# Where a weight table's comparisons run: VectorE or GpSimd

## The chip, the cores and the metric

The kernel runs on one core of a Trainium2 chip. A core has five engines that run side by side, each with its own instruction queue: TensorE (PE, matrix products), VectorE (DVE), ScalarE (ACT), GpSimd (POOL) and SyncE (SP, here the issuer of all transfers). The metric is the device time of one execution in microseconds; before the change its median is 2431.11 us over 3 runs (2429.63 to 2433.48).

## The reference, cut to what matters

Two "macaron" transformer layers act on x of 1024 tokens by 256 features. Each layer is a half-weighted feed-forward, an attention, and the same feed-forward again. The second layer's feed-forward does not store its weights: each weight is one of 16 values of a table `lut`, chosen by an index.

```
def _ghost_linear(x, idx, lut):
    w = lut[idx]
    return jnp.einsum('bsh,oh->bso', x, w)
gate = _ghost_linear(x, gate_idx, lut)
up = _ghost_linear(x, up_idx, lut)
h = jax.nn.silu(gate) * up
return _ghost_linear(h, down_idx, lut)

x = x + 0.5 * L0_ffn(layernorm(x))
x = x + L0_attn(layernorm(x))        # 16 heads of 128, window of 64, differential softmax, rope
x = x + 0.5 * L0_ffn(layernorm(x))
x = x + 0.5 * L1_ffn(layernorm(x))   # the table weights above
x = x + L1_attn(layernorm(x))        # gated delta rule
x = x + 0.5 * L1_ffn(layernorm(x))
```

The gate and up indices are 256 by 688, the down index 688 by 256 (padded to 768 rows in the kernel).

## The kernel before, in words

All of x stays in SBUF as eight tiles of 128 tokens. Matrix products work on 512 tokens at a time (a "half"). The layers follow each other in program order. Within each engine a planner at build time has laid out one fixed order of instructions, moving some of them past each other, and the engines synchronise by semaphores.

**The tables.** `lut_weights` (L169) is a Python generator that builds the three weight matrices `w1g`, `w1u` and `w1d`. It takes 14 pieces: for each of the two 128-row blocks of gate and up, one of 512 columns and one of 176, and for down six blocks of 256 columns. For each piece it loads the int32 index tile `ix` (two buffers, a transfer of SyncE, L178). Then, for each of the 16 table values k, one instruction compares all indices with k and multiplies the result by the value `lk` (L183, on VectorE); its output `eq` (three buffers) is added to the piece on GpSimd (L185). For k = 0 the comparison writes the piece itself and there is no addition. This makes 224 comparisons (64 of 512 columns, 64 of 176, 96 of 256) and 210 additions (60, 60 and 90).

**Where the steps go.** `lut_steps(columns)` advances the generator until about so many columns have been emitted. It is called after each of the 12 inner chunks of the first feed-forward with 1024, and after each chunk of attention with 1536, so the table work is spread behind the first feed-forward and the first attention. What is left is emitted after attention. The tables are read first in the fourth of the six parts.

**Around them.** In the first feed-forward, TensorE makes `pg` and `pu` (L135), ScalarE applies silu (L140), VectorE multiplies into `hT` (L143), TensorE makes `po` (L160) and VectorE adds it to x (L167). Then the layernorm runs on VectorE (L106 to L116) with transposes on TensorE and copies on ScalarE. The attention makes the values `v` (L212, copied by ScalarE in L219, shifted by transfers in L220 and L222). For each of four head groups it then makes one key and four query ropes per half of the tokens, ten in all: a product `pr` (L228, two buffers), three VectorE instructions (L237, L238, L240) and one GpSimd addition of `rot` (two buffers) in L241. After that come eight chunks per head group: scores `ps` on TensorE (L277), their maximum on VectorE (L288), exponentials on ScalarE (L294), the difference `d` of two softmaxes (L311, L314, two buffers), and its normalisation on GpSimd (L321). Transposes, the product with `v` and the output product end a chunk (L324, L329, L340, L347). GpSimd thus has attention's L241 and L321 in the same queue as the table additions.

After the attention come the remaining feed-forwards and the delta rule, which takes most of the span and has no table work.

Of the kernel before, what the change touches and what calls it, by code (L numbers as in the profile page):

```python
# [14 lines left out]
ALU = mybir.AluOpType  # L15
# [42 lines left out]
def macaron_kernel(ctx, tc, out, a):  # L58
    nc = tc.nc
# [109 lines left out]
    def lut_weights(pool):  # L169

        for src, dst in (("gate_idx", w1g), ("up_idx", w1u), ("down_idx", w1d)):
            for c in range(dst.shape[1]):
                for c0 in range(0, dst.shape[2], 512):
                    n = min(512, dst.shape[2] - c0)
                    ix = pool.tile([P, n], I32, name="ix", tag="ix", bufs=2)
                    nc.sync.dma_start(out=ix, in_=a[src][c * P : (c + 1) * P, c0 : c0 + n])  # L178
                    acc = dst[:, c, c0 : c0 + n]
                    for k in range(NLUT):  # L180
                        lk = bc[:, B_LUT + k : B_LUT + k + 1]
                        to = acc if k == 0 else pool.tile([P, n], F32, name="eq", tag="eq", bufs=3)
                        nc.vector.tensor_scalar(to, ix, float(k), lk, ALU.is_equal, ALU.mult)  # L183
                        if k:
                            nc.gpsimd.tensor_add(acc, acc, to)  # L185
                        yield n
# [164 lines left out]
    with tc.tile_pool(name="w0", bufs=1, side="right") as w0p:  # L351
# [12 lines left out]
        with tc.tile_pool(name="wa", bufs=1) as wap, tc.tile_pool(  # L364
# [19 lines left out]
            for i in range(2):  # L384
                nc.sync.dma_start(
                    out=wa["lam"][i * 64 : (i + 1) * 64, :], in_=lams[i].partition_broadcast(64)
                )
            lut = lut_weights(lutp)
            with ExitStack() as st:
                pools = stage_pools(st)  # L390
# [506 lines left out]
```

## Time and profile before

| | |
|---|---|
| median of 3 runs | 2431.11 us |
| profiled execution, own time | 2426.46 us |
| its span | 2424.6 us |
| busy TensorE, VectorE, ScalarE, GpSimd | 2093.0, 1431.5, 896.1, 854.9 us |
| comparisons L183 on VectorE | 175.65 us, from 39.9 to 276 us |
| first rope addition on GpSimd (L241) | 188.4 us |
| last table addition ends | 277.3 us |
| mean granted TensorE clock | 0.911 |

The page gives busy times of engines over one execution. A group line names the source line, the engine, the operation, output and inputs, the shapes and the count, and then the busy time, the mean of one in ns, and the engine's idle time before it with what ended it. The timeline gives start, duration and the number of merged instructions, with the idle time before in brackets. The windows view cuts the span into stretches and gives each engine's busy time there, the granted clock, and the share and rate of transfers.

### The profile page before, as it was taken

How to read it: one execution, taken by the hardware profiler on the slowest of the kernel's cores; microseconds unless marked ns; L12 is line 12 of the kernel's file. 1: busy time of each engine (PE TensorE's matmuls, PEld its weight loads, DVE VectorE, ACT ScalarE, POOL GpSimd, SP SyncE). 2: the span in 40 equal slices, each digit the busy share in tenths (PEclk: the TensorE clock that was granted, in tenths of full speed). 3: DMA queues.
4: the chain of work that ended last, by engine and by line, in shares of the span. 5: the costliest groups of instructions: out<-in, count | busy, mean ns of one | idle time of the engine just before them, and what ended most of it. 6: DMA issues, size and time to landing. Idle time of an engine off the chain costs nothing. (4 is left out here: it accounts for less than half of the span.)

```text
span 2424.6 us, 33184 instructions
## 1 busy us (share of the span) xinstructions
PE 2093.0 (86%) x12640; PEld 1714.2 (71%) x12640; DVE 1431.5 (59%) x3036; ACT 896.1 (37%) x1960; POOL 854.9 (35%) x995
## 2 busy tenths in 40 slices
PE   8535888878987898999889999799999979999989
PEld 4212554554546898888788888688888968888864
DVE  5999765553335565665655656556565655655541
ACT  2012453462233434343443343443434344343330
POOL 3887522210003334343243334334334233342320
PEclk9777898989997998999899989899998988988999
DMA  5010000000000000000000000000000000000000
GB/s 178 12 45 5 11 1 0 9 31 0 1 0 1 1 1 1 27 5 5 10 1 1 10 23 1 14 1 1 1 19 14 1 14 1 1 1 1 1 1 18
DMA packets 19182, 28.52 MB, mean 12 GB/s; under 512 B 2768, under 2 KB 11664, under 8 KB 18768
## 3 DMA queue, kind: packets, MB, share of 16 engines
q1 hardware_dynamic: 19024, 26.40, 3.5%
q8 instruction: 101, 1.65, 0.3%
q14 instruction: 57, 0.47, 0.1%
HBM read 23.38 MB, written 1.05 MB: 10 GB/s over the span
## 5 line engine op out<-in xcount | busy, mean ns | idle before, releaser
L652 PE MATMUL pm<-kq,k 128*128 128x128 f32 x1792 | 303.3, 302 | 90.8 <-POOL k L670 85.7
L670 POOL TENSOR_TENSOR k<-k,d 128x256 f32<-128x256 f32 x192 | 181.1, 943 | 497.9 <-PE pm L652 496.6
L699 PE MATMUL dz<-zt,mz 128*128 128x64 f32 x1792 | 342.5, 283 | 3.2 <-ACT mz L687 3.2
L652 PEld LDWEIGHTS pm<-kq,k 128*128 128x128 f32 x1792 | 254.4, 207 | 113.8 <-POOL k L670 104.7
L687 ACT COPY mz<-pmz 128x512 f32<-128x512 f32 x224 | 130.9, 584 | 502.7 <-PE pmz L685 502.7
L692 PE MATMUL dz<-mz,zt 128*128 128x64 f32 x1536 | 302.1, 279 | 5.1 <-ACT mz L687 4.8
L699 PEld LDWEIGHTS dz<-zt,mz 128*128 128x128 f32 x1792 | 279.6, 201 | 6.1 <-ACT mz L687 4.7
L685 PE MATMUL pmz<-z,mt 128*128 128x128 f32 x1792 | 271.9, 297 | 1.9 <-DVE z L709 1.9
L692 PEld LDWEIGHTS dz<-mz,zt 128*128 128x128 f32 x1536 | 248.4, 199 | 25.5 <-ACT mz L687 13.4
L685 PEld LDWEIGHTS pmz<-z,mt 128*128 128x128 f32 x1792 | 246.2, 209 | 10.8 <-DVE z L709 8.4
L664 DVE TENSOR_TENSOR kq<-kq,d 128x512 f32<-128x512 f32 x192 | 160.2, 835 | 126.5 <-PE pm L652 118.5
L709 DVE TENSOR_TENSOR z<-z,dz 128x256 f32<-128x256 f32 x192 | 80.7, 420 | 179.5 <-PE dz L699 178.9
L183 DVE TENSOR_SCALAR eq<-ix,bc 128x256 f32<-128x256 int32 (+2 forms) x210 | 165.9, 838 | 1.2 <-POOL w1g L185 0.4
L294 ACT ACTIVATE e<-ps,nm 128x128 f32<-128x128 f32 x256 | 90.6, 373 | 86.5 <-DVE nm L289 82.9
L680 DVE COPY_PREDICATED qk<-kon,pm 128x256 f32<-128x256 int32 x224 | 114.1, 510 | 0.0
L560 DVE SCALAR_TENSOR_TENSOR k<-ps,pp,k 128x256 f32<-128x256 f32 x192 | 87.2, 476 | 42.4 <-ACT k L558 40.4
L711 DVE TENSOR_TENSOR zt<-zt,dz 128x256 f32<-128x256 f32 x224 | 92.9, 415 | 28.4 <-PE dz L699 27.6
L560 DVE SCALAR_TENSOR_TENSOR v<-ps,pp,v 128x256 f32<-128x256 f32 x192 | 88.5, 478 | 15.5 <-ACT v L558 13.9
L560 DVE SCALAR_TENSOR_TENSOR q<-ps,pp,q 128x256 f32<-128x256 f32 x192 | 89.7, 479 | 13.3 <-ACT q L558 10.2
L546 PE MATMUL ps<-xnT,wk 128*128 128x259 f32 x256 | 77.6, 424 | 20.0 <-DVE k L560 20.0
L679 DVE TENSOR_TENSOR mt<-pm,kon 128x256 f32<-128x256 f32 x224 | 92.7, 414 | 0.0
L228 PE MATMUL pr<-xnT,wq 128*128 128x512 f32 x128 | 64.0, 629 | 29.4 <-DVE kT L240 27.0
(183 smaller groups left out, 4159.6 us busy)
## 6 DMA issues: line engine op xcount, KB each, us to landing
wq<-in_aWq SPq DMA_DIRECT2D x1, 2048.0 KB, 14.8
wo<-in_aWo SPq DMA_DIRECT2D x1, 2048.0 KB, 18.9
wk<-in_dWk SPq DMA_DIRECT2D x4, 512.0 KB, 3.8
wq<-in_dWq SPq DMA_DIRECT2D x4, 512.0 KB, 3.6
wv<-in_dWv SPq DMA_DIRECT2D x4, 512.0 KB, 3.6
wdo<-in_dWo SPq DMA_DIRECT2D x4, 512.0 KB, 3.8
v<-v SPq DMA_DIRECT2D x15, 128.0 KB, 2.3
x<-in_x SPq DMA_DIRECT2D x4, 256.0 KB, 3.2
```

What stands on the lines that cost most here:

```text
L183: nc.vector.tensor_scalar(to, ix, float(k), lk, ALU.is_equal, ALU.mult)
L560: nc.vector.scalar_tensor_tensor(yh, xi, pp[:, col : col + 1], yh, ALU.mult, ALU.add)
L652: nc.tensor.matmul(pm[:, h].rearrange("p b (s l) -> p b s l", l=n), lhsT=k[:, h, :], rhs=kq[:, :, h, :].rearrange("p b (s two l) -> p b s ...
L664: nc.vector.tensor_mul(kqr, kqr, dl.unsqueeze(1).unsqueeze(3).to_broadcast([P, 2, HG * runs, n]),)
L670: nc.gpsimd.tensor_mul(kl, kl, dr.unsqueeze(2).to_broadcast([P, HG * runs, n]))
L679: nc.vector.tensor_mul(dst(mt), src(0), mask4)
L680: nc.vector.copy_predicated(dst(qk), heads(mask.bitcast(I32)).rearrange("p h (s l) -> p h s l", l=n), src(1))
L685: nc.tensor.matmul(pmz[:, h, :], lhsT=mt[:, h, :], rhs=z[:, h, :], start=True, stop=True)
L687: nc.scalar.copy(mz, pmz)
L692: nc.tensor.matmul(dz[:, 0, h, :].rearrange("p (s l) -> p s l", l=n), lhsT=zt[:, h, :], rhs=left(mz[:, h, :], n), start=True, stop=True,)
L699: nc.tensor.matmul(dz[:, 1, h, :].rearrange("p (s l) -> p s l", l=n), lhsT=mz[:, h, :], rhs=right(zt[:, h, :], n), start=True, stop=True,)
L711: nc.vector.tensor_sub(zr, zr, runs4(dz[:, 1]))
```

## The change

The comparison with multiplication (L183) is issued on GpSimd in place of VectorE. Piece sizes, buffers, index loads, additions and the calls of `lut_steps` stay.

```
                     for k in range(NLUT):
                         lk = bc[:, B_LUT + k : B_LUT + k + 1]
                         to = acc if k == 0 else pool.tile([P, n], F32, name="eq", tag="eq", bufs=3)
-                        nc.vector.tensor_scalar(to, ix, float(k), lk, ALU.is_equal, ALU.mult)
+                        nc.gpsimd.tensor_scalar(to, ix, float(k), lk, ALU.is_equal, ALU.mult)
                         if k:
                             nc.gpsimd.tensor_add(acc, acc, to)
                         yield n
```

In the built program, VectorE's queue has no table instruction left. GpSimd's queue has the comparison of step k+1 between the additions of steps k-1 and k. The first rope addition L241 now stands behind 58 comparisons and 53 additions of 512 columns and 48 and 45 of 176 (before: behind 60 additions of 512, 60 of 176 and 23 of 256); the six first L321 of the first head group still stand before the end of the tables.

More of the change, by code (lines that the diff above doesn't have):

```diff
@@ L182, in lut_weights @@
                         to = acc if k == 0 else pool.tile([P, n], F32, name="eq", tag="eq", bufs=3)
-                        nc.vector.tensor_scalar(to, ix, float(k), lk, ALU.is_equal, ALU.mult)
+                        nc.gpsimd.tensor_scalar(to, ix, float(k), lk, ALU.is_equal, ALU.mult)
                         if k:
```

## The prediction

> **What bounds the kernel now.** The page says TensorE is busy 86% of the span, but the change acts only on the tables, so I first asked where they are built. The grouped list by shape for GpSimd, cut to 40 to 293 us, holds all of its table work (columns: count, busy us, mean ns, idle before it and what ended that):
>
> ```profile
> L185 POOL TENSOR_TENSOR w1d<-w1d,eq 128x256 f32<-128x256 f32 x90 | 66.2, 736 | 13.3 <-DVE eq L183 6.1 <-DVE nm L289 1.4 <-DVE lw L307 0.3
> L185 POOL TENSOR_TENSOR w1u<-w1u,eq 128x512 f32<-128x512 f32 x30 | 40.7, 1356 | 3.6 <-DVE eq L183 1.8
> L185 POOL TENSOR_TENSOR w1g<-w1g,eq 128x512 f32<-128x512 f32 x30 | 40.2, 1341 | 44.0 <-DVE eq L183 42.2
> L185 POOL TENSOR_TENSOR w1g<-w1g,eq 128x176 f32<-128x176 f32 x30 | 17.5, 582 | 2.6 <-DVE eq L183 0.6
> L185 POOL TENSOR_TENSOR w1u<-w1u,eq 128x176 f32<-128x176 f32 x30 | 17.1, 571 | 2.3 <-DVE eq L183 0.2
> ```
>
> So 210 additions, 181.7 us, and little idle time between them. The comparisons that feed them are on VectorE, 224 of them; the windows view of L183 alone sums to 175.65 us there, nothing after 300 us. Which engine sets the pace up to then? The windows view of the whole core (busy us of TensorE, its weight loads, VectorE, ScalarE, GpSimd, then the granted clock):
>
> ```profile
> 50.00:190.00 140.00, 68.48 (x160) 32.51 (x161) 138.99 (x187) 15.75 (x27) 125.02 (x141) 0.74 0.10 25
> 190.00:293.00 103.00, 71.95 (x291) 42.73 (x290) 91.72 (x191) 42.35 (x207) 69.24 (x85) 0.79 0.03 10
> 293.00:560.00 267.00, 215.96 (x955) 130.87 (x954) 153.32 (x406) 128.56 (x632) 63.08 (x55) 0.90 0.03 10
> ```
>
> From 50 to 190 us VectorE works 138.99 of 140 us and GpSimd 125.02. TensorE, at 68.48, waits. This is the second half of the first feed-forward, its layernorm, and the values of attention. VectorE is the bound, GpSimd close behind. After 293 us there is no table work. Last I took GpSimd's timeline at the hand-over, since what attention needs from it stands in the same queue:
>
> ```profile
> 181.32 6.37 POOL L185 TENSOR_TENSOR w1d<-w1d,eq 128x256 f32<-128x256 f32 x8 [0.23 <-DVE eq L183]
> 188.44 1.27 POOL L241 TENSOR_TENSOR kT<-kT,rot 128x512 f32<-128x512 f32 x1 [0.75 <-DVE kT L240]
> ...
> 228.54 1.09 POOL L321 TENSOR_TENSOR d<-d,dz 128x512 f32<-128x512 f32 x1
> 229.59 2.25 POOL L185 TENSOR_TENSOR w1d<-w1d,eq 128x256 f32<-128x256 f32 x3
> ...
> 275.62 1.65 POOL L185 TENSOR_TENSOR w1d<-w1d,eq 128x256 f32<-128x256 f32 x2 [0.43 <-DVE nm L289]
> 279.01 1.04 POOL L321 TENSOR_TENSOR d<-d,dz 128x512 f32<-128x512 f32 x1 [1.75 <-DVE dz L320]
> ...
> 291.45 1.04 POOL L321 TENSOR_TENSOR d<-d,dz 128x512 f32<-128x512 f32 x1 [5.00 <-DVE dz L320]
> ```
>
> The reader should see three dates: the first rope addition (L241) at 188.4, the last table addition ending at 277.3, the eighth and last normalisation (L321) of the first head group ending at 292.5. That last date is my yardstick. What follows it does not change, so the change is worth what it moves this date.
>
> [...] The trace has no comparison on GpSimd; its two-input addition of 512 takes 1.26 us, its copy (L646) 611 ns. [...] the 176-column comparison takes 298 ns at least and 714 on average beside the additions. [...] independent neighbours overlap: the addition after the L321 of 228.54 (ending at 229.63) starts at 229.59.
>
> **The change, step by step.** Removed from VectorE: 224 comparisons, 175.65 us. Added to GpSimd: the same 224, 64 of 512 columns, 64 of 176, 96 of 256. The built order puts the comparison of step k+1 between the additions of steps k-1 and k, and mostly ahead of the same rope and normalisation instructions as before.
>
> *Price of one comparison.* From below: the copy, one input and no arithmetic, 0.611 us at 512. The mean squares pass (L571, 1024 columns, 1.935 us) against the 512-column one (L758, 1.039) puts about 0.145 us of an instruction in its fixed part, so a copy-like comparison costs 0.38 at 256 and 0.30 at 176; 64x0.611+64x0.30+96x0.38 = 94.8 us. From above: the addition itself, 1.26, 0.72, 0.55: 184.8 us[...]. I take 0.85, 0.50 and 0.40, an estimate[...]. Sum 54.4+25.6+48.0 = 128.0 us.
>
> *Price of the additions now.* Without the comparisons contending: 1.26 (the single 512-column rows at 82 to 85 us read 1.27 to 1.30), 0.552 and 0.721, the least of each that the line's answer gives. 60x1.26+60x0.552+90x0.721 = 173.6 us, 8.1 less than before.
>
> *Waits.* [...] the eight of 181.32 take 6.37 us, 0.80 each, 75 ns over their 721. Now a comparison lies between, and about 0.04 us of each instruction overlaps its neighbour: 453 instructions up to the end of the tables, 19.0 us saved. If that overlap were lost on the 210 additions it would cost about 210x0.12 = 25 us, kept for the range.
>
> *Sum for the queue.* Start 39.9 (the index tile lands then, as before) + 128.0 + 173.6 + ten L241 at 1.27 + six L321 at 1.05 + three memsets, 0.8 − 19.0 = 342.3 us for the end of the tables. On the way: 58 comparisons and 53 additions of 512, 48 and 45 of 176 precede the first L241, which falls at about 192 (188.4 before); the tenth at 240 (211.4); the first L321 at 265 (228.5). The seventh L321 is then ready, the eighth needs its d buffer from the sixth and comes some 6 us after it, the spacing that the trace shows at 279 to 291. It ends at about 346 instead of 292.5: **+54 us**.
>
> *What is hidden.* VectorE's relief: feed-forward, layernorm and values finish earlier (TensorE's 68.5 us of work no longer stretch over 140), and the first two ropes then sit in the two rot buffers until about 192, because L241 is queued behind the tables. This gain is costed at nothing, its cover being GpSimd's queue; were GpSimd quick it would be worth up to some 70 us at the first rope (140 − 68.5). The fourteen index loads stay; SyncE now issues the last ones later, and some copies of v stand behind them. The last of them waits until the sixth piece is compared, about 173 us, and v is first read after 265: nothing; if the load were late, a few us. Memsets wait for VectorE, which is ahead. The tables are first used after 560 us, far later than 342. From the ninth L321 on, VectorE, ScalarE and TensorE set the pace as now.
>
> Against the profiled execution: span 2424.6 + 54 = 2478.6, its own time 2426.46 + 54 = 2480.5. The median of the runs is 4.65 us above that execution, so the predicted time is 2431.1 + 54 = 2485.
>
> **The rivals.** The shift is C − 74, C being the summed comparisons: (39.9 + C + 174.4 + 4) − 292.5.
> (a) *Copy-like comparison*: C about 95 to 110, time 2452 to 2467. For it: one input stream. Against: two arithmetic steps and a scalar read.
> (b) *Addition-like or worse*: C = 185, 2542[...]. For it: the addition runs at 2.1 ns per column, slower than the multiplication's 1.75[...].
> (c) *VectorE's relief wins*, on the other side: the 50 to 293 us stretch gets shorter because VectorE was its bound. It decides where C falls below 74 us, a mean of 0.33 us per comparison; at 0.25 us, C = 56 and the time 2413. Against: that mean is below the copy's, and VectorE itself, undisturbed, needs 0.30 to 0.48.
> That the change is not made can be ruled out from the built order: VectorE has no table instruction left.
>
> **How the numbers follow.** Chances: main forecast, 40 to 85 us longer, 0.50 (own range 2470 to 2516); (a), up to 40 longer, 0.22; (b) above 85, 0.21, of which 0.07 beyond 140; (c) 0.05; no change 0.02. A tenth left out below ends near +12 (2443), a tenth above near +135 (2566). TensorE's clock, 0.74 in the stretch that now idles more, may add or take 10 us. Faster by over 0.2% is (c), 0.05; within 0.2%, about what a measurement of this kernel can tell from no change, 0.02; slower 0.93.
>
> **What would show it.** Right: GpSimd almost without a gap from 40 to about 340 us; the first L241 near 192; the 512-column comparison near 0.85 us; rope on VectorE waiting on GpSimd before 190; VectorE well under half busy there; the stretches after the eighth L321 as long as before. Wrong: comparisons under 0.4 us or an order of execution with gaps of GpSimd before L321 would mean that another engine bounds; a changed clock after 350 us would mean that the shift is not additive.

## The result and the profile after

The changed kernel takes 2695.25 us, the median of 4 runs (2693.95 to 2699.09), against 2430.37 for the kernel before, run beside it. The ratio is 1.1093 (95% interval 1.1074 to 1.1113). The forecast was 2485, with a range up to 2566: the direction was right, the size five times too small. The profiled execution took 2695.45 us (span 2693.7), so its span is 269.1 us longer than that of the kernel before.

First, the page of the kernel after: the busy time of each engine, and two of its rows of 40 slices (67.3 us each, busy tenths).

```profile
PE 2083.6 (77%) x12624; PEld 1710.9 (64%) x12640; DVE 1261.4 (47%) x2812; ACT 895.6 (33%) x1960; POOL 1139.7 (42%) x1219
PE   8500212368788988899998999998999998999989
POOL 4999999942120003433423424423424423433420
```

VectorE lost 170 us of work (1431.5 before) and GpSimd gained 285 (854.9 before). The 285 stand in one block: GpSimd is full in slices 2 to 8, and beneath it TensorE falls from 5 tenths in slice 2 to between 0 and 3 tenths in the others.

The windows view of the kernel after, with the same cuts as the one shown of before, and one more stretch, from the end of the eighth L321 to the end (busy us of TensorE, its weight loads, VectorE, ScalarE, GpSimd, then the granted clock):

```profile
50.00:190.00 140.00, 56.33 (x157) 27.01 (x156) 16.98 (x34) 13.55 (x25) 131.90 (x114) 0.72 0.02 5
190.00:293.00 103.00, 0.00 (x0) 0.00 (x0) 0.00 (x0) 0.00 (x0) 97.79 (x83) 0.50 0.10 23
293.00:560.00 267.00, 76.26 (x262) 45.89 (x266) 47.37 (x109) 39.40 (x195) 246.30 (x254) 0.59 0.02 5
...
564.60:2693.70 2129.10, 1907.19 (x12073) 1614.55 (x12084) 1175.94 (x2608) 827.95 (x1708) 652.09 (x759) 0.93 0.02 6
```

The same last stretch in the kernel before:

```profile
292.50:2424.60 2132.10, 1913.77 (x12084) 1618.36 (x12084) 1176.48 (x2608) 827.88 (x1708) 651.58 (x758) 0.93 0.02 6
```

From 190 to 293 us no engine works but GpSimd. And after the eighth L321 the two kernels are the same to 3 us in 2130. The whole loss lies ahead of that date, which moved from 292.5 to 564.6, by 272.1 us.

What GpSimd does in that time: its grouped list by shape in the kernel after, 30 to 620 us (count, busy us, mean ns, idle before it).

```profile
L183 POOL TENSOR_SCALAR eq<-ix,bc 128x512 f32<-128x512 int32 x60 | 120.1, 2003 | 4.7
L183 POOL TENSOR_SCALAR eq<-ix,bc 128x256 f32<-128x256 int32 x90 | 103.0, 1146 | 7.1
L185 POOL TENSOR_TENSOR w1d<-w1d,eq 128x256 f32<-128x256 f32 x90 | 65.5, 728 | 5.3
L183 POOL TENSOR_SCALAR eq<-ix,bc 128x176 f32<-128x176 int32 x60 | 52.6, 877 | 4.7
L185 POOL TENSOR_TENSOR w1g<-w1g,eq 128x512 f32<-128x512 f32 x30 | 37.9, 1264 | 1.8
```

A comparison of 512 columns takes 2.00 us, more than the addition that follows it. With the 14 comparisons for k = 0, which write the piece itself, the 224 comparisons make 64 x 2.003 + 64 x 0.877 + 96 x 1.146 = 294.3 us. The additions sum to 174.7.

GpSimd's timeline in the kernel after (start, duration, instruction, number merged, idle time before in brackets), at the start of the tables, at the first rope addition and at the hand-over:

```profile
46.96 2.00 POOL L183 TENSOR_SCALAR eq<-ix,bc 128x512 f32<-128x512 int32 x1
48.92 1.26 POOL L185 TENSOR_TENSOR w1g<-w1g,eq 128x512 f32<-128x512 f32 x1
50.28 2.15 POOL L183 TENSOR_SCALAR eq<-ix,bc 128x512 f32<-128x512 int32 x1
52.52 1.26 POOL L185 TENSOR_TENSOR w1g<-w1g,eq 128x512 f32<-128x512 f32 x1
...
303.27 1.26 POOL L241 TENSOR_TENSOR kT<-kT,rot 128x512 f32<-128x512 f32 x1
...
553.03 1.53 POOL L185 TENSOR_TENSOR w1d<-w1d,eq 128x256 f32<-128x256 f32 x2
555.03 1.04 POOL L321 TENSOR_TENSOR d<-d,dz 128x512 f32<-128x512 f32 x1 [0.39 <-DVE dz L320]
563.59 1.04 POOL L321 TENSOR_TENSOR d<-d,dz 128x512 f32<-128x512 f32 x1 [7.52 <-DVE dz L320]
```

The three dates of the forecast are there: first L241 at 303.3 (188.4 before), tables' end at 554.6 (277.3), eighth L321 ended at 564.6 (292.5). Between the early neighbours there are small holes: the addition of 48.92 ends at 50.18, the next comparison starts at 50.28.

Who stands and waits meanwhile: the waits view of the kernel after, 40 to 570 us (waiting instruction, what it waited for, total us, count, the longest).

```profile
ACT L294 <- DVE nm L289: 264.1, 1, 264.1
PE pr L228 <- DVE qT L240: 204.9, 4, 196.3
DVE rot L237 <- POOL kT L241: 204.7, 2, 196.2
```

Read from below, these are one chain: VectorE's third rope product needs a `rot` buffer, which the first L241 on GpSimd has yet to release; TensorE's next rope product waits for VectorE, and ScalarE's first exponential for the scores after it. All of them wait for one instruction that stands behind table work in GpSimd's queue.

### The profile page after: what moved, and what is told of

It reads as the page before. It is cut to its first block, busy times and chain, and to the rows that moved or that the text cites. A ratio compares the mean times of both kernels' runs of the same rounds, so it can differ in the third digit from the quotient of the medians.

```text
span 2693.7 us, 32979 instructions
## 1 busy us (share of the span) xinstructions
PE 2083.6 (77%) x12624; PEld 1710.9 (64%) x12640; DVE 1261.4 (47%) x2812; ACT 895.6 (33%) x1960; POOL 1139.7 (42%) x1219
## 5 line engine op out<-in xcount | busy, mean ns | idle before, releaser
L183 POOL TENSOR_SCALAR eq<-ix,bc 128x256 f32<-128x256 int32 (+2 forms) x210 | 275.6, 1314 | 16.5
L228 PEld LDWEIGHTS pr<-xnT,wq 128*128 128x128 f32 x128 | 23.9, 204 | 238.7 <-issue 227.7
L237 DVE TENSOR_TENSOR rot<-pr,sin 64x512 f32<-64x512 f32 x40 | 27.7, 693 | 274.2 <-POOL kT L241 204.7
L324 PE MATMUL pd<-kon,d 128*128 128x128 f32 x128 | 25.2, 329 | 151.2 <-POOL d L321 150.8
L324 PEld LDWEIGHTS pd<-kon,d 128*128 128x128 f32 x128 | 17.3, 167 | 158.7 <-POOL d L321 157.4
## 6 DMA issues: line engine op xcount, KB each, us to landing
v<-v SPq DMA_DIRECT2D x15, 128.0 KB, 2.3
```

Source lines behind the costliest of these rows:

```text
L183: nc.gpsimd.tensor_scalar(to, ix, float(k), lk, ALU.is_equal, ALU.mult)
L228: nc.tensor.matmul(pr, lhsT=w[:, c, hcol : hcol + HD], rhs=xnT[:, c, PAD + hf * 512 : PAD + (hf + 1) * 512], start=(c == 0), stop=(c == KC ...
```

## The experiments

The first question was the price: the comparison costs 2.00 us where the forecast had 0.85. The second was whether that price, with the queue behind it, accounts for the whole 272 us. The third was what would happen with the additions on VectorE too. Unless another base is named, a diff is against the kernel after. All ratios are to the kernel before, run on the same chip.

| experiment | median us | ratio [95%] |
|---|---|---|
| after | 2695.25 | 1.1093 [1.1074, 1.1113] |
| three forms of comparison | 2612.04 (one run) | – |
| four eq buffers | 2689.26 | 1.1081 [1.1044, 1.1119] |
| multiply-add in place of every comparison | 2519.64 | 1.0399 [1.0379, 1.0418] |
| additions on VectorE, comparisons on GpSimd | 2539.23 | 1.0464 [1.0440, 1.0487] |
| both on VectorE | 2324.96 | 0.9581 [0.9556, 0.9607] |
| both on VectorE but the down additions | 2360.68 | 0.9729 [0.9714, 0.9743] |
| after, tables spread later | 2663.16 | 1.0974 [1.0958, 1.0990] |
| before, tables spread later | 2446.24 | 1.0080 [1.0064, 1.0097] |

### What in the comparison costs 2 us

Four causes were possible: the second arithmetic step with its per-partition scalar, the int32 input, the comparison itself, or GpSimd being slow here whatever it runs. Each table got another form.

```
-    nc.gpsimd.tensor_scalar(to, ix, float(k), lk, ALU.is_equal, ALU.mult)
+    if src == "gate_idx":
+        nc.gpsimd.tensor_scalar(to, ix, float(k), None, ALU.is_equal)
+    elif src == "up_idx":
+        nc.gpsimd.tensor_scalar(to, ix.bitcast(F32), float(k), lk, ALU.is_equal, ALU.mult)
+    else:
+        nc.gpsimd.tensor_scalar(to, ix, float(k), lk, ALU.mult, ALU.add)
```

> The changed kernel with three forms of the GpSimd comparison, one per table, so that its tables do not hold the right weights: gate compares only (one step, no multiplication, no pointer scalar), up reads the same index bits as float32 instead of int32, down keeps int32 and two steps but multiplies and adds instead of comparing. The changed kernel's row is 2.00 us at 512 columns, 1.15 at 256, 0.88 at 176. Theory 1, the second step or the pointer scalar makes the loop slow: gate falls to about 1.15 at 512 and 0.58 at 176, the other two stay. Theory 2, the int32 input does: up falls to about 1.0 and 0.5, the others stay. Theory 3, the comparison does: down falls to about 0.7, gate stays. Theory 4, [...]: all three stay. By my queue account each us saved in the comparisons takes a us off the total: about 2658 us under 1 or 2, 2652 under 3, 2695 under 4.

GpSimd's grouped list of this kernel, 30 to 560 us (L184 is gate, L186 up, L188 down):

```profile
L186 POOL TENSOR_SCALAR eq<-ix,bc 128x512 f32<-128x512 f32 x30 | 59.8, 1996 | 2.3
L184 POOL TENSOR_SCALAR eq<-ix 128x512 f32<-128x512 int32 x30 | 44.7, 1492 | 2.0
L188 POOL TENSOR_SCALAR eq<-ix,bc 128x256 f32<-128x256 int32 x90 | 43.9, 489 | 7.0
L184 POOL TENSOR_SCALAR eq<-ix 128x176 f32<-128x176 int32 x30 | 19.4, 648 | 2.0
```

The same bits read as float32 take 1.996 us against 2.003: the input type costs nothing. Without the second step the 512-column form falls to 1.492, so that step, with its scalar, is worth 0.5 us. A multiplication and an addition on int32, with the same per-partition scalar, take 0.489 us at 256 columns where the comparison takes 1.146. It is the form with the comparison that is dear. None of the four theories holds alone: gate fell too, but to 1.49 us and not to 1.15, and the total lies 40 us below the lowest that was expected (2652). Whether the cost is the comparison's own, or whether multiply-add is quicker than most pairs of operations, no run tells apart: no other pair was tried. From two widths of each form come slopes: comparison and multiplication (2003 − 877) / 336 = 3.35 ns per column, comparison alone (1492 − 648) / 336 = 2.51.

Here the comparisons sum to 207.4 us, the tables end at 466.5 and the eighth L321 at 476.3.

### Is the price the whole shift?

Here the price alone is changed: every comparison becomes a multiply-add, with the same order of instructions.

```
-    nc.gpsimd.tensor_scalar(to, ix, float(k), lk, ALU.is_equal, ALU.mult)
+    nc.gpsimd.tensor_scalar(to, ix, float(k), lk, ALU.mult, ALU.add)
```

> The changed kernel with all 224 comparisons on GpSimd replaced by the cheap two-step form (multiply by k, add the table value), so that its tables do not hold the right weights; order, waits and buffers stay. It asks whether my sum was right apart from the price: the cheap form costs 0.49 us at 256 columns, so about 0.77 at 512 and 0.40 at 176, some 122 us in all, near the 128 us that I had forecast for the comparisons. Theory, the queue account with the measured gaps: 2695 less the difference of 294 and 122 us, 2515 to 2535 us; my forecast, 2485, plus the 45 us of gaps that it had as overlap gives the same. Rival, a further term is wrong [...]: then the time is off this by more than 20 us.

GpSimd's grouped list of this kernel, 30 to 560 us:

```profile
L183 POOL TENSOR_SCALAR eq<-ix,bc 128x256 f32<-128x256 int32 x90 | 43.8, 488 | 7.0
L183 POOL TENSOR_SCALAR eq<-ix,bc 128x512 f32<-128x512 int32 x60 | 41.6, 695 | 4.7
```

With 0.416 us at 176 columns the sum is 64 x 0.695 + 64 x 0.416 + 96 x 0.488 = 117.9 us. The eighth L321 ends at 387.9 us, 95.4 later than before, and the total is 95.8 longer (2519.64 against 2423.82), inside what was expected. Three kernels now lie on one line: comparisons of 117.9, 207.4 and 294.3 us put the eighth L321 at 387.9, 476.3 and 564.6. The slopes are 88.4 / 89.5 = 0.99 and 88.3 / 86.9 = 1.02. Each microsecond of comparison moves the date, and with it the end, by one microsecond. This is the queue of the forecast, and it shows the forecast's second error too: with a summed price of 117.9, below the 128.0 that was forecast, the shift is 95 us and not 44 (117.9 − 74). The other 51 us are the waits, with the late eighth L321.

### The holes between comparison and addition

In the kernel after, a comparison mostly starts 98 ns after the addition before it (so in 162 of 205 such pairs), and an addition 80 ns after the comparison before it (153 of 191). The other pairs overlap by 15 to 40 ns; over all pairs the means are 75 and 57 ns, 26 us in all. Two comparisons that stand next to each other mostly overlap by 22 ns (15 of 18). A comparison that waits for its `eq` buffer could explain the holes, and a fourth buffer would shorten such a wait.

```
-    to = acc if k == 0 else pool.tile([P, n], F32, name="eq", tag="eq", bufs=3)
+    to = acc if k == 0 else pool.tile([P, n], F32, name="eq", tag="eq", bufs=4)
```

> The changed kernel with four eq buffers instead of three; the order of the instructions stays. It asks where the 80 to 98 ns between neighbouring comparisons and additions on GpSimd come from (about 26 us in all, where I had forecast an overlap of 19 us). If the reuse of eq buffers made each comparison wait for the addition before it, most gaps become overlaps and the time falls by 20 to 40 us, to 2655 to 2675. If the gap belongs to the alternation of the two instructions or to the waits on GpSimd's own semaphore, nothing changes: 2690 to 2700.

2689.26 us, and the holes are still 98 and 80 ns; the interval of the ratio holds that of the kernel after. It is not the buffers. The built program says the same: of the 224 comparisons only the first of each piece has a wait, for its index load, and none waits for an addition. What makes the holes stays open: the trace shows them where a comparison and an addition alternate, after the first pairs of a piece, and the views name no releaser for idle times this short.

### The additions on VectorE instead

The opposite split: the comparisons stay on GpSimd and the additions go to VectorE. The queue alone would then give about 2498; mutual blocking of the two engines would add to it, up to 2575.

```
-    nc.gpsimd.tensor_add(acc, acc, to)
+    nc.vector.tensor_add(acc, acc, to)
```

> The changed kernel with the 210 additions moved from GpSimd to VectorE; the comparisons stay on GpSimd. Theory of the queue: the loss is the length of GpSimd's queue ahead of attention's L241 and L321. It loses 175 us of additions and most gaps, so the eighth L321 ends at about 39.9 + 294 + 22 + 4 to 10, some 360 us, 68 us later than before the change: about 2498 us. Rival, [...] each two-input addition on VectorE (0.3 to 0.6 us) holds up a comparison for its whole length, some 80 us more: about 2575 us. Rival, the loss has nothing to do with the queue (clock, other engines): stays near 2695 us.

GpSimd's grouped list of this kernel, 30 to 500 us:

```profile
L183 POOL TENSOR_SCALAR eq<-ix,bc 128x512 f32<-128x512 int32 x60 | 143.4, 2392 | 5.4 <-DVE nm L289 0.7
```

2539.23 us, between the two. The 512-column comparison goes from 2003 to 2392 ns, the 256 from 1146 to 1323, the 176 from 877 to 1014; all of them from 294.3 to 345.0 us. So the two engines running side by side cost GpSimd 51 us, and the time stands about half-way between the two forecasts. The eighth L321 ends at 373.0 us, 80 later than before the change, where the theory of the queue had 68; the rest of the 112 us (2539.23 against 2427.26) comes after that date, while the tables last until 459 us, in the second head group.

### Everything on VectorE

```
-    nc.gpsimd.tensor_scalar(to, ix, float(k), lk, ALU.is_equal, ALU.mult)
+    nc.vector.tensor_scalar(to, ix, float(k), lk, ALU.is_equal, ALU.mult)
...
-    nc.gpsimd.tensor_add(acc, acc, to)
+    nc.vector.tensor_add(acc, acc, to)
```

> Both the comparisons and the additions on VectorE, none of the tables on GpSimd. VectorE then carries comparisons at their undisturbed 0.48, 0.34 and 0.30 us, 83 us in all, and additions, by the 256-column L709 and the 512-column L240 some 0.69, 0.41 and 0.30 us, 96 us in all: 179 us, against 176 us that the comparisons alone take there in the kernel before because GpSimd's additions block them. [...] about the time of the kernel before or a little less, 2410 to 2440 us, since L241 and L321 no longer stand behind table work on GpSimd. Rival, VectorE is the bound and has all of the additions on top of its 176 us: about 90 us slower than before, 2520 us.

2324.96 us, ratio 0.9581 [0.9556, 0.9607]: 102 us faster than the kernel before, where 2410 to 2440 was expected. VectorE's grouped list of this kernel, 30 to 400 us:

```profile
L183 DVE TENSOR_SCALAR eq<-ix,bc 128x512 f32<-128x512 int32 x60 | 29.0, 494 | 0.0
L183 DVE TENSOR_SCALAR eq<-ix,bc 128x256 f32<-128x256 int32 x90 | 32.9, 378 | 0.0
L185 DVE TENSOR_TENSOR w1d<-w1d,eq 128x256 f32<-128x256 f32 x90 | 40.8, 453 | 0.0
```

The first of these lines in VectorE's list of the kernel before:

```profile
L183 DVE TENSOR_SCALAR eq<-ix,bc 128x512 f32<-128x512 int32 x60 | 67.6, 1172 | 0.0
```

The comparison of 512 columns falls from 1172 to 494 ns, that of 256 from 697 to 378, that of 176 from 714 to 349, as soon as GpSimd has no additions. VectorE's whole table work, additions included, keeps it busy for 172.5 us (overlaps counted once), where its comparisons alone kept it busy for 175.65 before; in sums of durations it is 193.6 against 187.5. So taking over the additions cost VectorE about nothing. And less of the work stands ahead of attention: 49.9 us before the first rope on VectorE, against 131.6 us in the kernel before. The windows view of this kernel:

```profile
50.00:190.00 140.00, 119.53 (x453) 66.88 (x453) 130.64 (x354) 54.38 (x232) 22.73 (x22) 0.91 0.09 22
```

TensorE works 119.5 of 140 us there, against 68.5 before and 56.3 after. The first L241 starts at 104.4 us and the eighth L321 ends at 185.8, 106.7 earlier than before, so the gain is made by then. The tables last until 394 us, spread over the head groups, which start at 104.4, 193.6, 280.0 and 364.8. The expectation had the amount about right, 179 us, with the comparisons at their undisturbed price. What it left out is the place: it did not ask how much of this amount the planner would still put ahead of the first rope.

### Does an addition on GpSimd really block the comparison on VectorE?

The test is to give back to GpSimd only the 90 additions of the down table. If they hold up VectorE for as long as they take there (65.5 us in the kernel after), nothing is gained. Base: the kernel with both on VectorE.

```
-    nc.vector.tensor_add(acc, acc, to)
+    (nc.gpsimd if src == "down_idx" else nc.vector).tensor_add(acc, acc, to)
```

> All tables on VectorE except the 90 additions of the down table, which go to GpSimd. With all tables on VectorE that engine is busy 44 to 49 us of every 50 up to 400 us, GpSimd 10 to 16. Theory, VectorE is the bound there: 41 us of additions leave it, the time falls by 10 to 30 us below 2325, to 2295 to 2315 us. Rival, [...] no gain or a loss, 2325 to 2350 us.

VectorE's grouped list of this kernel, 186 to 360 us:

```profile
L183 DVE TENSOR_SCALAR eq<-ix,bc 128x256 f32<-128x256 int32 x90 | 60.7, 714 | 0.9 <-POOL w1d L185 0.9
```

The same stretch of the kernel with both on VectorE:

```profile
L183 DVE TENSOR_SCALAR eq<-ix,bc 128x256 f32<-128x256 int32 x79 | 29.2, 383 | 0.0
```

The 256-column comparisons double, from 383 to 714 ns, and wait for almost nothing; those of 512 and 176 columns, whose additions stayed on VectorE, keep 496 and 350 ns. So an addition on GpSimd does lengthen the comparison on VectorE; in the opposite split VectorE's additions cost GpSimd's comparisons 51 us. By what way the two engines hold each other up, no run shows.

The kernel is 36 us slower than the one with all on VectorE, although VectorE has 90 instructions less, and slower than either expectation. The lengthening alone does not explain this: VectorE's table work still sums to less than before the additions left it, 184.6 against 193.6 us. Attention's L241 and L321 again share GpSimd's queue with additions, and TensorE's weight loads (L324) wait 38.0 us for L321 from 186 to 410 us, where they waited 22.9. How the 36 us divide was not measured.

### Amount or position?

If the tables only stood at the wrong place in GpSimd's queue, spreading them would help. A one-column copy from x into the index tile, which the load then overwrites, makes each index load wait for the latest finished chunk of attention. (Lines after it lie three or more lower: L241 is L244, L321 is L324.)

```
     ix = pool.tile([P, n], I32, name="ix", tag="ix", bufs=2)
+    if ticket:
+        nc.vector.tensor_copy(ix[:, 0:1], ticket[-1])
...
     nc.vector.tensor_add(x[:, n, :], x[:, n, :], po)
+    ticket.append(x[:, n, 0:1])
     lut_steps(1536)
```

> The changed kernel's engines (comparisons and additions on GpSimd), but each index load that is asked for during attention must first wait for the chunk of attention behind which it was asked for: a one-column copy of x into the index tile on VectorE, overwritten by the load. So the same table work stands later in GpSimd's queue, spread over the four head groups; in the built order some 32 comparisons of 512 and 16 of 176 are ahead of the first L241 instead of 58 and 48. It tells the position of the work from its amount. Theory of position: attention no longer waits for the whole of the tables, the first L241 falls near 175 us, and only the tables' own end, some 650 to 690 us with GpSimd's 495 us of table work and 84 us of attention, may hold the second layer's feed-forward, which began at 632 us before the change: 2440 to 2500 us. Rival, the amount: GpSimd has 294 us more to do before the tables are read, wherever it stands: near 2690 us.

2663.16 us: 32 us of 265 are won. The eighth normalisation now ends at 266.0 us, earlier than in the kernel before, but the tables last until 807.3. In between, clumps of up to 15 comparisons with 13 additions (22 us) stand ahead of a rope addition or a normalisation, and then GpSimd in turn waits for attention, as the waits view of this kernel shows (40 to 900 us):

```profile
POOL d L324 <- DVE dz L323: 123.5, 22, 8.4
...
ACT sg L140 <- POOL eq L185: 45.9, 1, 45.9
```

So 123.5 us of GpSimd's time go idle in 22 waits. One queue holds both in a fixed order, and each stalls for the other: TensorE's L327 in its turn waited 150.1 us for L324's `d`. This placement does not hide the amount. The second line is a wait that came with the edit: after attention the next feed-forward's silu (`sg`, L140) stands until a comparison (here L185) is through, though it reads no table. In the source the pool of the `eq` tiles closes before that feed-forward opens its own, so `sg` may take over their memory; this reason was not tested. Without the wait, by an estimate from its length, the kernel would have won some 46 us more, and would still have lost most of the 237 us that it lies behind the kernel before (2663.16 against 2426.10). The run also shows that the date of the eighth L321 is a yardstick only as long as nothing behind it changes.

The same edit in the kernel before, to see whether a later order alone gives what the kernel with all on VectorE won:

> The kernel before (comparisons on VectorE, additions on GpSimd) with the same waits of the index loads for attention's chunks. It asks why all tables on VectorE gained 102 us: there the planner also spread the table work to 394 us, while in the kernel before it is packed into 40 to 277 us. Theory of order: what counted is that feed-forward and rope are not behind table work; then this kernel too is faster by 70 to 110 us, 2320 to 2360 us. Rival, [...] the gain came from no longer having the two engines block each other; then this kernel gains little, 2390 to 2430 us.

2446.24 us, 20 us slower than before and outside both expectations. The first rope addition comes earlier, at 130.7 us, but the comparisons are nearly as slow as before (1071, 717 and 626 ns for 512, 256 and 176 columns, against 1128, 699 and 752, those of k = 0 counted in) and now stretch the head groups to 99 to 112 us apart. Attention's last L321 ends at 546.6 us, as before (546.1); the 20 us arise after it, where the tables last until 578.8. This later order without the faster comparisons wins nothing. How the 102 us divide between the two was not measured further.

## Why the prediction was wrong

The step that failed first is *Price of one comparison*, 128.0 us where the runs show 294.3, and then *Waits*, 19.0 us saved where 26 were lost. By the forecast's own sum for the eighth L321:

| term | forecast | measured | difference |
|---|---|---|---|
| summed comparisons C | 128.0 | 294.3 | +166.3 |
| overlap or holes between instructions | −19.0 | +26 | +45 |
| eighth L321 after the tables' end | 4 | 10.0 | +6 |
| additions | 173.6 | 174.7 | +1 |
| shift | +54 | +272 | +218 |

- **Price.** 0.85, 0.50 and 0.40 us were forecast; 2.00, 1.15 and 0.88 were measured. The three values were the author's estimate, which no trace showed; at 512 columns it lay between the copy's 0.611 us and the addition's 1.26. Rival (a), a copy-like comparison, was further off still. Rival (b), "addition-like or worse", had the right side, but its addition-like sum of 184.8 us was 109.5 too low. The comparison with multiplication takes 3.35 ns per column, against the addition's 2.1, and the line through its two widths gives 0.29 us for the fixed part, where the forecast had read 0.145 from the multiplication. The int32 input, the immediate and the pointer scalar do not explain it, since a multiply-add with all three takes 0.695 us. A reason to doubt the middle value lay in the forecast itself: its prices grow by (0.85 − 0.40) / 336 = 1.34 ns per column, less than both slopes that it had from the trace, the addition's 2.1 and the multiplication's 1.75. The chance given to anything beyond +140 us was 0.07.
- **Waits.** It was argued from independent neighbours, an addition behind a normalisation, which overlap by some 0.04 us, that comparisons and additions would overlap too. They mostly did not: 98 and 80 ns of idle time took the overlap's place. The hole ahead of an addition is even the same as in the kernel before, where 166 of 199 neighbouring additions stand some 78 ns apart; a comparison in between did not remove it. For losing the overlap the range kept 25 us, on the additions alone; the holes stand ahead of the comparisons as well, and the term was off by 45.
- **Hand-over.** The seventh L321 stands where it was forecast, just behind the tables; the eighth follows it after 8.6 us and not 6, waiting for its `dz`.
- **Start and additions.** Both held: 39.8 us against 39.9, 174.7 against 173.6.
- **Yardstick.** It held: the date moved by 272.1, the last instruction by 269.1, and the stretch between is the same to 3 us. TensorE's granted clock fell in the idle stretches (0.50 where it had no matmul), but took nothing from what follows, 0.93 in both.
- **VectorE's relief.** It was hidden, as argued: the gain at the rope products vanished behind GpSimd's queue. VectorE's timeline of the kernel after:

```profile
104.15 0.69 DVE L237 TENSOR_TENSOR rot<-pr,sin 64x512 f32<-64x512 f32 x1 [17.97 <-PE pr L228]
304.56 0.69 DVE L237 TENSOR_TENSOR rot<-pr,sin 64x512 f32<-64x512 f32 x1 [196.18 <-POOL kT L241]
```

The rope products are under way at 104 us, far ahead of before, and then VectorE stands for 196 us behind GpSimd's queue. Rival (c), in which this relief wins, needed a mean of 0.33 us per comparison; the measured mean is 294.3 / 224 = 1.31.

- **The index loads and the copies of v** cost nothing, as forecast: the products with v (L329) waited 16.6 us for `dT` and for no transfer.
- **What the forecast did not ask** is where the additions should run. It saw that they block VectorE's comparisons, 298 ns against 714, and used this only to price the additions. The kernel with all on VectorE shows what it was worth.

## What to carry to other kernels

Before work is moved to an engine, get a measured price of that very operation there: a copy, an addition and a comparison of 512 columns differ by more than three times on GpSimd (0.61, 1.26 and 2.00 us), and bounds built from neighbours should be given the chance that the spread among them suggests. Where an engine's queue also holds short instructions that other engines need, each microsecond put ahead of them can be paid in full: it was here, one for one over three kernels (slopes 0.99 and 1.02), since it was that queue that ended last. And look at how an instruction's duration differs from its least: VectorE's comparisons were twice as long as need be because of their helper on GpSimd (1172 against 494 ns for 512 columns), and taking the helper away left VectorE no busier with the tables (172.5 against 175.65 us) and, with the order that the planner then laid out, made the kernel 4.2% faster.

## What the runs showed of the hardware that was not expected

- On GpSimd a comparison with multiplication is much dearer than a multiplication with addition in one instruction: 2.00 against 0.695 us for 512 columns of the same int32 input. The slopes are 3.35, 2.51 and 0.83 ns per column for comparison with multiplication, comparison alone, and multiply-add. The last is less than half of the 2.1 ns of the addition of two tiles.
- The int32 input of these instructions cost nothing against float32 (2.003 and 1.996 us).
- GpSimd mostly overlapped neighbouring comparisons by 22 ns, but mostly left 80 to 98 ns between a comparison and an addition that alternate; a further buffer did not change it.
- VectorE and GpSimd slow each other both ways: GpSimd's additions lengthened VectorE's 256-column comparison from 383 to 714 ns, VectorE's additions GpSimd's 512-column one from 2003 to 2392.
